# A four-layer graph network in float32: merging feature chunks for half of the nodes, two rows at a time

## The chip, the cores and the metric

The kernel runs on one core of one Trainium2 chip. The core has a matrix engine (TensorE, PE in the profile), a vector engine (VectorE, DVE), a scalar engine (ScalarE, ACT), a general one (GpSimd, POOL) and a queue for transfers (SyncE, SP). They run side by side and wait for each other by semaphores. The metric is the device time of one execution in microseconds (us).

## The reference, cut to what matters

x holds 64 graphs of 256 nodes with 128 features. Each of four layers does x = x + f(relu(layernorm(x)), adj). The first is the costly one: it takes a LeakyReLU of 256 values for every pair of nodes.

```python
def _L0_gnn_ref(x, W, b_lin, a, bias):        # x: normalised nodes; W = bias = adj
    W1, W2 = (W[:, :F], W[:, F:])              # F = 128, 256 outputs
    s1 = jnp.einsum('bkf,ef->bke', x, W1)
    s2 = jnp.einsum('bkf,ef->bke', x, W2)
    pre = s1[:, :, None, :] + s2[:, None, :, :] + b_lin
    h = jnp.where(pre >= 0, pre, ALPHA * pre)  # ALPHA = 0.2
    e = jnp.einsum('bije,e->bij', h, a) + bias
    attn = jax.nn.softmax(e, axis=2)
    out = jax.nn.sigmoid(jnp.einsum('bij,bjf->bif', attn, x))
    return out
...
h = jnp.maximum(_layernorm(x, axis=-1), 0.0)
x = x + _L0_gnn_ref(h, adj, L0_gnn_b_lin, L0_gnn_a, adj)
```

Layers 1 and 2 are attention layers on the same nodes, layer 3 is a gated recurrent cell with five steps that multiplies by adj in each. All is float32.

## The kernel before, in words

**The pair values.** With 0.2 x taken out as a linear term, what is left of the LeakyReLU is 0.8 relu(s1 + s2 + b). The kernel scales the 256 features by |a| (in `w_p`), so each counts with weight +0.8 or -0.8. It sorts them by sign: `place` says where a feature goes, and places 2p and 2p + 1 become partition p of chunk 0 and of chunk 1. The two features of a pair then have one sign, but for one pair where the number of positive ones is odd. For a node i, a *tile* is 128 features x 256 nodes j. ACT makes it as relu(s2 + s1[i]) (L687), POOL and DVE as max(s2, -s1[i]) (L692, L669), which differs by a number that falls out of the softmax over j.

**Batches.** A graph's 256 nodes are 32 rows of 8: four groups g of 32 nodes in each of two blocks `ic` of 128. A *batch* is one chunk of one row: a buffer `r` of 4 x 2 tiles, 8 KB on each partition, of which there are `BUFS` = 11. TensorE multiplies it by the signs: four matmuls (L740) side by side, one for each g, of 128 x 32 by 128 x 512, where the 512 are both blocks. `a_win` holds the signs in a window of zeros, so that row t of each group gets the sum. Every batch of a graph adds to the same bank `e_ps`.

**Merging.** Where five batches or more (`SPARE`) wait for TensorE as a row is begun (`Pairs.begin`), the row is *merged*: only chunk 0 is made, and DVE then makes chunk 1 of each of the eight tiles and adds it onto chunk 0 in one instruction, max(s2, -s1) + r (L709, in `merge`). TensorE has one batch to multiply instead of two. This needs one sign for both features of a pair. In the odd pair, the feature that has the place n_pos, in chunk 1, therefore gets size 0 in the permutation (`a_abs1`), and its part comes back by a rank-one correction: a matmul `left_ps`, and min(left, bound) + adj into `adj_l` (L570), one instruction for each block, which softmax0 then adds (L755).

**The order of work** is written out by a planner inside the kernel (`Model`, `Chain` and the loop at the end). It keeps a clock for each of PE, DVE, ACT and POOL, with fixed costs (a tile 365 ns on ACT and 454 on POOL, 2198 for DVE's eight, 1131 for its four, a merge 392, a batch 858), and issues next whatever can start first. Tiles are handed out in half batches to whichever of ACT, POOL and DVE is free and finds a buffer. All other work comes in chains: `ahead` (norms, s1, s2 and corrections of the next graphs), `behind` (softmax of the graph before), `chain12` (layers 1 and 2), `chain3` (layer 3; chains 4 and 5 for the last two groups). A chain's steps are spaced by a pace, 2400 ns for layer 3, until the last two graphs are begun. Each engine runs its instructions in the order written.

**Groups and transfers.** Graphs go in groups of two (one in the first two and last two groups). `load_x` fetches a group's x into one of five buffers, three groups ahead, from `begin`. SP holds all loads of x, the stores of the outputs, and the small transfers of the corrections' bounds, in order.

```python
merged = waiting >= SPARE
for ec in range(1 if merged else 2):
    batch = {"t": self.row, "ec": ec, "merged": merged, "halves": 0, "ready": 0.0}
    self.todo += [(batch, ec, 0), (batch, ec, 1)]
self.row += 1
```

Of the kernel before, what the change touches and what calls it, by code (L numbers as in the profile page):

```python
# [8 lines left out]
F32 = mybir.dt.float32  # L9
# [7 lines left out]
FLT_MAX = 3.4028234663852886e38  # L17
STEPS = 5
INV_SQRT_D = 1.0 / (128.0 ** 0.5)
BUFS = 11  # L20
SPARE = 5
MARGIN = {"pe": 300}
LANDS = 3400
# [32 lines left out]
def kernel(ctx: ExitStack, tc: tile.TileContext, ins: dict, out: bass.AP):  # L56
# [69 lines left out]
        return t[firsts[g] : firsts[g] + GROUPS[g]].rearrange("b (c p) f -> p (b c) f", p=P)  # L126

    def load_x(g):
        xt = ap.tile([P, 2 * GROUPS[g], P], F32, tag="xt", name="xt", bufs=5)
        nc.sync.dma_start(out=xt, in_=of_group(x, g))  # L130
        return xt

# [73 lines left out]
    bm_bc = fetch([P, P], "bm_bc", ins["L1_gnn_bm"].partition_broadcast(P))  # L206
    be_bc = fetch([P, 1], "be_bc", ins["L1_gnn_be"].partition_broadcast(P))
    biases = {k: column("L3_gnn_" + k) for k in ("w3_b", "u3_b", "w4_b", "w5_b", "u5_b")}
    xts.append(load_x(2))


    adj_t = constant([P, 2, N], "adj_t")
# [7 lines left out]
    def constants0():  # L220
# [34 lines left out]
        last, a_abs1 = col("last"), col("a_abs1")  # L255
        dve(2).tensor_scalar(last, place, n_pos, None, ALU.is_equal)
        dve(2).tensor_tensor(a_abs1, a_abs, last, ALU.mult)
        dve(2).tensor_tensor(a_abs1, a_abs, a_abs1, ALU.subtract)
        perm = lent([P, 2, 2, P], "perm", "e_t", 2)
        for src in range(2):  # L260
            for c, size in ((0, a_abs), (1, a_abs1)):
                dve(P).tensor_scalar(
                    perm[:, src, c, :], places[:, c, :], place[:, src : src + 1],
                    size[:, src : src + 1], ALU.is_equal, ALU.mult,
                )
        yield "pe"
        b_ps = psum([P, 2], "blin_ps")
# [50 lines left out]
        dve(1).tensor_copy(odd_all, p)  # L318
        left, left_n, left_nb = col("left"), col("left_n"), col("left_nb")
        dve(2).tensor_tensor(left, a_col, last, ALU.mult)  # L320
        dve(2).tensor_scalar(left, left, odd_all, 0.8, ALU.mult, ALU.mult)
        dve(2).tensor_scalar(left_n, left, -1.0, None, ALU.mult)
        dve(2).tensor_tensor(left_nb, left_n, blin, ALU.mult)
        for c in range(2):
# [105 lines left out]
    def ln_relu(space, xt, tag, ln, when=None, at=None):  # L430

        G = xt.shape[1]
        for g in range(G):
            if g % 2 == 0:
                yield "dve", when, at
            if g == 0:
                st = sp.tile([P, G, 6], F32, tag=tag + "_st", name="bst", bufs=2)
                mv = sp.tile([P, G, 2], F32, tag=tag + "_mv", name="bmv", bufs=2)
# [6 lines left out]
        ve = sp.tile([P, G], F32, tag=tag + "_ve", name="bve", bufs=2)  # L445
        minus = sp.tile([P, G], F32, tag=tag + "_mm", name="bmm", bufs=2)
        pool(277).tensor_scalar(ve, mv[:, :, 1], 1.0, LN_EPS, ALU.mult, ALU.add)
        pool(150).tensor_scalar(minus, mv[:, :, 0], -1.0, 0.0, ALU.mult, ALU.add)
        rstd = sp.tile([P, G], F32, tag=tag + "_rs", name="brs", bufs=2)
        pool(1085).tensor_tensor(rstd, ve, neg_half[:, 0:G], ALU.pow)  # L450
        shift = sp.tile([P, G], F32, tag=tag + "_sh", name="bsh", bufs=2)
# [81 lines left out]
    def bounds(of):  # L533


        yield "pe", lambda: counts["left"] > 0
        h_t = of["h_t"]
        G = h_t.shape[1]
        p = psum_h([P, P], "bound_ps")
        model.op("pe", P * 1.676)  # L540
        for c in range(G):
            nc.tensor.matmul(
                p[bass.ts(c, 32), :], lhsT=left_w, rhs=h_t[:, c, :], start=True, stop=True
            )
        yield "act"
        rows = sp.tile([P, P], F32, tag="rows", name="rows", bufs=2)
        act(P, 1).activation(
            rows[0 : 32 * G, :], p[0 : 32 * G, :], AF.Identity, bias=left_b[0 : 32 * G, :]
        )
        row = dp.tile([G, P], F32, tag="row", name="row")  # L550
        for c in range(G):
            nc.sync.dma_start(out=row[c : c + 1, :], in_=rows[32 * c : 32 * c + 1, :])
        bound = sp.tile([P, G], F32, tag="bound", name="bound")
        nc.sync.dma_start(out=bound, in_=row.rearrange("c p -> p c"))
        of["bound"] = bound
        of["bound_at"] = model.t["act"] + MEMORY

    def senders(b, of, to):
# [27 lines left out]
    class Pairs:  # L586

        def __init__(self, g, b, of, snd):
            self.g, self.b, self.of, self.snd = g, b, of, snd
            self.row = 0
# [6 lines left out]
            self.s1n_v = of["s1n"][:, :, bass.ts(b, N)].rearrange(  # L600
                "p c (k g t) -> p c g k t", k=2, g=4
            )

        def more(self):
            return self.todo or self.row < 32
# [4 lines left out]

        def begin(self):
            waiting = sum(x["halves"] == 2 for x in self.batches)
            merged = waiting >= SPARE
            for ec in range(1 if merged else 2):
                batch = {"t": self.row, "ec": ec, "merged": merged, "halves": 0, "ready": 0.0}
                self.todo += [(batch, ec, 0), (batch, ec, 1)]
            self.row += 1

        def finished(self):

# [21 lines left out]
            batch["halves"] += 1  # L642
            batch["ready"] = max(batch["ready"], model.t[who] + LAG[who])

        def nodes(self, t, g2):

            return [
                (g, ic, self.b * N + ic * P + 32 * g + t)
                for g in (2 * g2, 2 * g2 + 1) for ic in range(2)
            ]  # L650

        def make(self, who):
# [10 lines left out]
            if who == "dve":  # L663
                whole = g2 == 0 and self.todo and self.todo[0][0] is batch
                if whole:
                    self.todo.pop(0)
                n = 4 if whole else 2
                model.op("dve", model.WHOLE if whole else model.HALF)
                nc.vector.tensor_tensor(  # L669
                    r[:, 2 * g2 : 2 * g2 + n, :, :],  # L670
                    s2[:, ec : ec + 1, :].unsqueeze(1).to_broadcast([P, n, 2, N]),
                    self.s1n_v[:, ec, 2 * g2 : 2 * g2 + n, :, t : t + 1].to_broadcast([P, n, 2, N]),
                    ALU.max,
                )
                if whole:
# [25 lines left out]
        def merge(self):  # L701

            _, batch, g2 = self.merges.pop(0)
            r, t = batch["r"], batch["t"]
            for g, ic, i in self.nodes(t, g2):
                if g > 2 * g2 or ic:
                    yield
                model.op("dve", model.MERGE)
                nc.vector.scalar_tensor_tensor(  # L709
# [20 lines left out]
        def multiply(self):  # L730
# [5 lines left out]
            self.over = not self.batches and not self.more()  # L736
            t, r = batch["t"], batch["r"]
            model.op("pe", model.BATCH)
            for g in range(4):
                nc.tensor.matmul(  # L740
                    self.e_ps[bass.ts(g, 32), :, :].rearrange("p a b -> p (a b)"),
                    lhsT=a_win[:, batch["ec"], 31 - t : 63 - t], rhs=flat(r[:, g, :, :]),
                    start=False, stop=self.over, skip_group_check=True,
                )

    def softmax0(g, b, of, e_ps, snd):

# [2 lines left out]
        for ic in range(2):  # L750
            yield "dve", lambda: "adj_l" in snd

            if ic == 0:
                nmax = sp.tile([P, 2], F32, tag="nmax", name="nmax")
            dve(N, more=10).tensor_tensor_reduce(  # L755
                e_ps[:, ic, :], e_ps[:, ic, :], snd["adj_l"][:, ic, :], -1.0, FLT_MAX,
                ALU.add, ALU.min, nmax[:, ic : ic + 1],
            )
        for ic in range(2):
# [529 lines left out]
```

## Time and profile before

| | before |
|---|---|
| runs shown | 5033.29, 5038.96, 5039.4 us |
| median | 5038.96 us |
| the profiled execution | 5032.98 us, its span 5031.1 us |
| TensorE clock granted | 0.999 |
| matmuls of batches (L740) | 13912, of 512 columns each (27824 records) |
| tiles made by ACT / POOL | 10248 / 10100 |
| made by DVE (L669) | 659 of eight tiles, 551 of four |
| merges on DVE (L709) | 4944 |

How to read it: the page gives busy time and share of the span for each engine, and then groups of instructions by source line, with the number, the busy time, the mean time of one, and the time the engine stood idle just before them, with what ended it. Each float32 matmul leaves two records. ACT's and TensorE's instructions overlap their neighbours, so the mean time of one is longer than the step from one to the next. The table by stage gives busy time for each engine in a stretch of the span; the timeline gives the instructions in order of time, equal neighbours put together.

### The profile page before, as it was taken

The page shows a single profiled execution, that of the slowest core. Times are in us where ns is not written, and L with a number is a line of the kernel's source. Part 1 is how long each engine was busy: PE and PEld are TensorE (multiplying, and loading weights), DVE is VectorE, ACT ScalarE, POOL GpSimd, SP SyncE. Part 2 cuts the span into 40 slices and gives each one's busy share as a digit, 9 for nine tenths or more (in the row PEclk, how much of TensorE's full clock was granted, in tenths as well). Part 3 has the DMA queues.
Part 4 walks back from the last instruction along what each step waited for, and adds up shares of the span by engine and source line. Part 5 has one row for each costly group of instructions (what it writes and reads, how often), then busy time and mean ns, then how long its engine had stood idle before and what let it go on. Part 6 is the DMA issues. An engine that isn't in the chain of part 4 may idle for free. (4 is left out here: it accounts for less than half of the span.)

```text
span 5031.1 us, 151796 instructions
## 1 busy us (share of the span) xinstructions
PE 4975.7 (99%) x57307; PEld 1949.9 (39%) x57307; DVE 4926.9 (98%) x9026; ACT 4945.2 (98%) x12984; POOL 4817.0 (96%) x10725
## 2 busy tenths in 40 slices
PE   9999999999999999999999999999999999999998
PEld 3334433333334333343333333333333443333433
DVE  9999999999999999999999999999999999999995
ACT  8999999999999999999999999999999999999995
POOL 8999999999999999999999999999999999999991
PEclk9999999999999999999999999999999999999999
DMA  0000000000000000000000000000000000000000
GB/s 23 4 5 2 5 6 6 6 2 6 6 6 6 2 6 6 6 6 2 6 6 6 6 2 6 6 6 6 4 6 6 6 4 3 5 4 4 4 4 8
DMA packets 56017, 28.02 MB, mean 6 GB/s; under 512 B 20336, under 2 KB 55280, under 8 KB 55280
## 3 DMA queue, kind: packets, MB, share of 16 engines
q1 hardware_dynamic: 54736, 18.04, 1.5%
q8 instruction: 449, 7.36, 0.6%
q14 instruction: 288, 2.36, 0.2%
q10 hardware_dynamic: 544, 0.26, 0.0%
HBM read 9.84 MB, written 8.45 MB: 4 GB/s over the span
## 5 line engine op out<-in xcount | busy, mean ns | idle before, releaser
L692 POOL TENSOR_SCALAR r<-s,s1n 128x256 f32<-128x256 f32 x10100 | 4567.7, 476 | 55.7 <-PE e_ps L740 28.0
L687 ACT ACTIVATE r<-s_act,s 128x256 f32<-128x256 f32 x9736 | 4360.0, 1073 | 4.6 <-PE e_ps L740 4.3
L740 PE MATMUL e_ps<-r,a_win 128*32 128x512 f32 x27824 | 3251.8, 593 | 8.8 <-DVE r L709 4.0
L669 DVE TENSOR_TENSOR r<-s_ps,s1n 128x2048 f32<-128x2048 f32 (+1 forms) x1210 | 2120.7, 1790 | 0.8 <-POOL r L692 0.8
L709 DVE SCALAR_TENSOR_TENSOR r<-s_ps,s1n,r 128x256 f32<-128x256 f32 x4944 | 2013.3, 471 | 0.2
L740 PEld LDWEIGHTS e_ps<-r,a_win 128*32 128x32 f32 x27824 | 918.8, 110 | 1721.4 <-issue 1290.3
L687 ACT ACTIVATE r<-s,s 128x256 f32<-128x256 f32 x512 | 318.8, 1234 | 0.0
L458 ACT ACTIVATE h<-x,bsh,brs 128x128 f32<-128x128 f32 x384 | 264.3, 1040 | 10.5 <-POOL bsh L452 5.0
L109 PE MATMUL m_ps<-adj_t,hn 128*32 128x256 f32 x4096 | 253.6, 381 | 1.1 <-ACT hn L1066 1.1
L1025 ACT ACTIVATE m_ps<-gate_ps,br 128x512 f32<-128x512 f32 (+1 forms) x170 | 194.7, 1145 | 14.2 <-PE gate_ps L109 13.1
L1045 ACT ACTIVATE hv_ps<-hv_ps,bh 128x512 f32<-128x512 f32 (+1 forms) x170 | 198.7, 1169 | 7.2 <-PE hv_ps L109 7.2
L1043 ACT ACTIVATE gate_ps<-gate_ps,bz 128x512 f32<-128x512 f32 (+1 forms) x170 | 203.8, 1200 | 1.1 <-PE gate_ps L109 1.1
L1015 ACT COPY m_t<-m_ps 128x512 f32<-128x512 f32 (+1 forms) x170 | 193.9, 1140 | 6.1 <-PE m_ps L109 5.6
L109 PEld LDWEIGHTS m_ps<-adj_t,hn 128*32 128x32 f32 x4096 | 140.0, 110 | 126.2 <-issue 46.1
L109 PE MATMUL gate_ps<-m_t,t_w_w 128*32 128x512 f32 (+1 forms) x1360 | 172.7, 572 | 2.6 <-ACT m_t L1015 2.2
L109 PE MATMUL gate_ps<-m_t,w_t 128*32 128x512 f32 (+1 forms) x1360 | 172.5, 568 | 2.5 <-ACT m_ps L1025 2.4
L109 PE MATMUL hv_ps<-rh,u_th 128*32 128x512 f32 (+1 forms) x1360 | 172.1, 567 | 2.1 <-DVE rh L1028 2.0
L109 PE MATMUL hv_ps<-m_t,t_w_w 128*32 128x512 f32 (+1 forms) x1360 | 172.4, 568 | 0.0
L1066 ACT COPY hn<-hn_ps 128x512 f32<-128x512 f32 (+1 forms) x136 | 153.2, 1127 | 8.7 <-PE hn_ps L116 8.6
L109 PE MATMUL gate_ps<-hf,u_t 128*32 128x512 f32 (+1 forms) x1088 | 141.9, 571 | 0.0
L109 PE MATMUL s_ps<-h0t,w_p 128*32 128x256 f32 (+1 forms) x1568 | 136.2, 446 | 1.2 <-ACT h0t L474 0.5
L450 POOL TENSOR_TENSOR brs<-bve,neg_half 128x4 f32<-128x4 f32 (+1 forms) x136 | 133.5, 982 | 0.0
(214 smaller groups left out, 4781.2 us busy)
## 6 DMA issues: line engine op xcount, KB each, us to landing
xt<-in_x_dram SPq DMA_DIRECT2D x30, 256.0 KB
out_dram<-y SPq DMA_DIRECT2D x30, 256.0 KB
row<-rows SPq DMA_DIRECT2D x128, 0.5 KB
xt<-in_x_dram SPq DMA_DIRECT2D x4, 128.0 KB
out_dram<-y SPq DMA_DIRECT2D x4, 128.0 KB
bound<-row SPq DMA_DIRECT2D x30, 2.0 KB
raw_L_gnn_w_w<-in_L_gnn_w_w_dram SPq DMA_DIRECT2D x3, 128.0 KB
adj_n<-in_adj_dram ACTq DMA_DIRECT2D x1, 256.0 KB
```

The costliest lines, as they stand in the source:

```text
L109: nc.tensor.matmul(out[bass.ts(c, 32), :], lhsT=lhsT[:, bass.ts(c, 32)], rhs=rhs, **flags)
L458: act(P, 2, 1).activation(h[:, g, :], xt[:, g, :], AF.Relu, bias=shift[:, g : g + 1], scale=rstd[:, g : g + 1],)
L669: nc.vector.tensor_tensor(r[:, 2 * g2 : 2 * g2 + n, :, :], s2[:, ec : ec + 1, :].unsqueeze(1).to_broadcast([P, n, 2, N]), self.s1n_v[:, ec ...
L687: nc.scalar.activation(r[:, g, ic, :], s2[:, ec, :], AF.Relu, bias=s1[:, ec, i : i + 1])
L692: nc.gpsimd.tensor_scalar(r[:, g, ic, :], s2[:, ec, :], FLT_MAX, s1n[:, ec, i : i + 1], ALU.min, ALU.max,)
L709: nc.vector.scalar_tensor_tensor(r[:, g, ic, :], self.own("dve")[:, 1, :], self.of["s1n"][:, 1, i : i + 1], r[:, g, ic, :], ALU.max, ALU.add,)
L740: nc.tensor.matmul(self.e_ps[bass.ts(g, 32), :, :].rearrange("p a b -> p (a b)"), lhsT=a_win[:, batch["ec"], 31 - t : 63 - t], rhs=flat(r[ ...
L1015: act(W).copy(m_t, m_ps)
L1025: act(W, 1).activation(t_r, g_ps, AF.Tanh, bias=br, scale=0.5)
L1043: act(W, 1).activation(t_z, g_ps, AF.Tanh, bias=bz, scale=0.5)
L1045: act(W, 1).activation(cand, hv_ps, AF.Tanh, bias=bh)
L1066: act(W).copy(hn, tp)
```

## The change

`BUFS` becomes 12. The space comes from x (four buffers, fetched two groups ahead), from `adj_l` (one block instead of two) and from small tiles with one buffer instead of two.

Merging is now done for the first block of nodes alone, and for two rows t and t + 1 at once. A merged pair of rows has three batches: chunk 0 of row t and chunk 0 of row t + 1, both blocks, onto whose first block DVE adds chunk 1 (four merges each); and one batch that holds chunk 1 of the second block for both rows. So eight merges still save one batch in four. A graph can merge at most half as much as before.

The odd pair's feature keeps its size. In the first block its chunk 1 always goes with chunk 0's sign, merged or not, and the correction (with 1.6 in place of 0.8) is made for that block alone. In the second block chunk 1 goes with its own sign, and needs none. So chunk 1 of a row that isn't merged has a different weight for each block, and is multiplied by eight matmuls of 256 columns in place of four of 512; so is the batch of two rows.

```diff
-BUFS = 11
+BUFS = 12
...
-        xt = ap.tile([P, 2 * GROUPS[g], P], F32, tag="xt", name="xt", bufs=5)
+        xt = ap.tile([P, 2 * GROUPS[g], P], F32, tag="xt", name="xt", bufs=4)
...
-    xts.append(load_x(2))
...
-        dve(2).tensor_tensor(a_abs1, a_abs, last, ALU.mult)
-        dve(2).tensor_tensor(a_abs1, a_abs, a_abs1, ALU.subtract)
...
-        dve(2).tensor_scalar(left, left, odd_all, 0.8, ALU.mult, ALU.mult)
+        dve(2).tensor_scalar(left, left, odd_all, 1.6, ALU.mult, ALU.mult)
...
-        for ic in range(2):
-            yield "dve", None, of["bound_at"]
-            if ic == 0:
-                adj_l = ap.tile([P, 2, N], F32, tag="adj_l", name="adj_l", bufs=3)
-            dve(N, 1).scalar_tensor_tensor(
-                adj_l[:, ic, :], p, of["bound"][:, 2 * b + ic : 2 * b + ic + 1], adj_n[:, ic, :],
-                ALU.min, ALU.add,
-            )
+        yield "dve", None, of["bound_at"]
+        adj_l = ap.tile([P, N], F32, tag="adj_l", name="adj_l", bufs=3)
+        dve(N, 1).scalar_tensor_tensor(
+            adj_l, p, of["bound"][:, 2 * b : 2 * b + 1], adj_n[:, 0, :], ALU.min, ALU.add
+        )
...
-            merged = waiting >= SPARE
-            for ec in range(1 if merged else 2):
-                batch = {"t": self.row, "ec": ec, "merged": merged, "halves": 0, "ready": 0.0}
+            merged = waiting >= SPARE and self.row < 31
+            t = self.row
+
+            if merged:
+                kinds = ((t, 0, True, False), (t + 1, 0, True, False), (t, 1, False, True))
+            else:
+                kinds = ((t, 0, False, False), (t, 1, False, False))
+            for t, ec, on_top, two in kinds:
+                batch = {
+                    "t": t, "ec": ec, "merged": on_top, "two": two, "halves": 0, "ready": 0.0
+                }
                 self.todo += [(batch, ec, 0), (batch, ec, 1)]
-            self.row += 1
+            self.row += 2 if merged else 1
...
-            for g, ic, i in self.nodes(t, g2):
-                if g > 2 * g2 or ic:
+            for g, ic, i in self.nodes(batch, g2):
+                if ic:
+                    continue
+                if g > 2 * g2:
                     yield
                 model.op("dve", model.MERGE)
...
-            for g in range(4):
-                nc.tensor.matmul(
-                    self.e_ps[bass.ts(g, 32), :, :].rearrange("p a b -> p (a b)"),
-                    lhsT=a_win[:, batch["ec"], 31 - t : 63 - t], rhs=flat(r[:, g, :, :]),
-                    start=False, stop=self.over, skip_group_check=True,
-                )
+
+            if batch["two"]:
+                parts = ((1, t, 1, 0), (1, t + 1, 1, 1))
+            elif batch["ec"]:
+                parts = ((0, t, 0, 0), (1, t, 1, 1))
+            else:
+                parts = ((slice(0, 2), t, 0, slice(0, 2)),)
+            for ic, t, sign, k in parts:
+                for g in range(4):
+                    to, of = self.e_ps[bass.ts(g, 32), ic, :], r[:, g, k, :]
+                    if len(parts) == 1:
+                        to, of = to.rearrange("p a b -> p (a b)"), flat(of)
+                    nc.tensor.matmul(
+                        to, lhsT=a_win[:, sign, 31 - t : 63 - t], rhs=of,
+                        start=False, stop=self.over, skip_group_check=True,
+                    )
...
-            if g + 3 < len(GROUPS):
-                xts.append(load_x(g + 3))
+            if g + 2 < len(GROUPS):
+                xts.append(load_x(g + 2))
```

Left out of the diff: the eight small statistics tiles and `rows` with one buffer instead of two, the views of s1 for a batch of two rows in `nodes` and `make`, and the reads of `adj_n` in place of `adj_l` for the second block in `softmax0`.

More of the change, by code (lines that the diff above doesn't have):

```diff
@@ L253, in constants0 @@
         dve(2).tensor_tensor(place, dif, neg_pl, ALU.add)
-        last, a_abs1 = col("last"), col("a_abs1")
+        last = col("last")
         dve(2).tensor_scalar(last, place, n_pos, None, ALU.is_equal)
-        dve(2).tensor_tensor(a_abs1, a_abs, last, ALU.mult)
-        dve(2).tensor_tensor(a_abs1, a_abs, a_abs1, ALU.subtract)
         perm = lent([P, 2, 2, P], "perm", "e_t", 2)
         for src in range(2):
-            for c, size in ((0, a_abs), (1, a_abs1)):
+            for c in range(2):
                 dve(P).tensor_scalar(
                     perm[:, src, c, :], places[:, c, :], place[:, src : src + 1],
-                    size[:, src : src + 1], ALU.is_equal, ALU.mult,
+                    a_abs[:, src : src + 1], ALU.is_equal, ALU.mult,
                 )
@@ L436, in ln_relu @@
             if g == 0:
-                st = sp.tile([P, G, 6], F32, tag=tag + "_st", name="bst", bufs=2)
-                mv = sp.tile([P, G, 2], F32, tag=tag + "_mv", name="bmv", bufs=2)
+                st = sp.tile([P, G, 6], F32, tag=tag + "_st", name="bst", bufs=1)
+                mv = sp.tile([P, G, 2], F32, tag=tag + "_mv", name="bmv", bufs=1)
             dve(P).bn_stats(st[:, g, :], xt[:, g, :])
@@ L443, in ln_relu @@
         yield "pool"
-        ve = sp.tile([P, G], F32, tag=tag + "_ve", name="bve", bufs=2)
-        minus = sp.tile([P, G], F32, tag=tag + "_mm", name="bmm", bufs=2)
+        ve = sp.tile([P, G], F32, tag=tag + "_ve", name="bve", bufs=1)
+        minus = sp.tile([P, G], F32, tag=tag + "_mm", name="bmm", bufs=1)
         pool(277).tensor_scalar(ve, mv[:, :, 1], 1.0, LN_EPS, ALU.mult, ALU.add)
         pool(150).tensor_scalar(minus, mv[:, :, 0], -1.0, 0.0, ALU.mult, ALU.add)
-        rstd = sp.tile([P, G], F32, tag=tag + "_rs", name="brs", bufs=2)
+        rstd = sp.tile([P, G], F32, tag=tag + "_rs", name="brs", bufs=1)
         pool(1085).tensor_tensor(rstd, ve, neg_half[:, 0:G], ALU.pow)
-        shift = sp.tile([P, G], F32, tag=tag + "_sh", name="bsh", bufs=2)
+        shift = sp.tile([P, G], F32, tag=tag + "_sh", name="bsh", bufs=1)
         pool(302).tensor_tensor(shift, minus, rstd, ALU.mult)
@@ L545, in bounds @@
         yield "act"
-        rows = sp.tile([P, P], F32, tag="rows", name="rows", bufs=2)
+        rows = sp.tile([P, P], F32, tag="rows", name="rows", bufs=1)
         act(P, 1).activation(
@@ L602, in __init__ @@
             )
+            self.s1n_b = of["s1n"][:, :, bass.ts(b, N)].rearrange(
+                "p c (k g t) -> p c k g t", k=2, g=4
+            )
         def more(self):
@@ L643, in whole, with nodes @@
             batch["ready"] = max(batch["ready"], model.t[who] + LAG[who])
-        def nodes(self, t, g2):
+        def nodes(self, batch, g2):
+            t, two = batch["t"], batch["two"]
             return [
-                (g, ic, self.b * N + ic * P + 32 * g + t)
-                for g in (2 * g2, 2 * g2 + 1) for ic in range(2)
+                (g, k, self.b * N + 32 * g + t + (P + k if two else k * P))
+                for g in (2 * g2, 2 * g2 + 1) for k in range(2)
             ]
@@ L667, in make @@
                 n = 4 if whole else 2
+                if batch["two"]:
+                    s1n = self.s1n_b[:, ec, 1, 2 * g2 : 2 * g2 + n, t : t + 2].unsqueeze(3)
+                else:
+                    s1n = self.s1n_v[:, ec, 2 * g2 : 2 * g2 + n, :, t : t + 1]
                 model.op("dve", model.WHOLE if whole else model.HALF)
@@ L671, in make @@
                     s2[:, ec : ec + 1, :].unsqueeze(1).to_broadcast([P, n, 2, N]),
-                    self.s1n_v[:, ec, 2 * g2 : 2 * g2 + n, :, t : t + 1].to_broadcast([P, n, 2, N]),
+                    s1n.to_broadcast([P, n, 2, N]),
                     ALU.max,
@@ L703, in merge @@
             _, batch, g2 = self.merges.pop(0)
-            r, t = batch["r"], batch["t"]
-            for g, ic, i in self.nodes(t, g2):
-                if g > 2 * g2 or ic:
+            r = batch["r"]
+            for g, ic, i in self.nodes(batch, g2):
+                if ic:
+                    continue
+                if g > 2 * g2:
                     yield
@@ L738, in multiply @@
             model.op("pe", model.BATCH)
-            for g in range(4):
-                nc.tensor.matmul(
-                    self.e_ps[bass.ts(g, 32), :, :].rearrange("p a b -> p (a b)"),
-                    lhsT=a_win[:, batch["ec"], 31 - t : 63 - t], rhs=flat(r[:, g, :, :]),
-                    start=False, stop=self.over, skip_group_check=True,
-                )
+            if batch["two"]:
+                parts = ((1, t, 1, 0), (1, t + 1, 1, 1))
+            elif batch["ec"]:
+                parts = ((0, t, 0, 0), (1, t, 1, 1))
+            else:
+                parts = ((slice(0, 2), t, 0, slice(0, 2)),)
[7 more added lines that the diff above has]
+                        start=False, stop=self.over, skip_group_check=True,
+                    )
     def softmax0(g, b, of, e_ps, snd):
@@ L755, in softmax0 @@
             dve(N, more=10).tensor_tensor_reduce(
-                e_ps[:, ic, :], e_ps[:, ic, :], snd["adj_l"][:, ic, :], -1.0, FLT_MAX,
+                e_ps[:, ic, :], e_ps[:, ic, :], adj_n[:, 1, :] if ic else snd["adj_l"], -1.0, FLT_MAX,
                 ALU.add, ALU.min, nmax[:, ic : ic + 1],
```

## The prediction

> **What bounds the kernel now.** I read the page first. All four engines are over 95% busy, so no engine is "the" bound by its share, and the chain that ended last says only how the last 94 us go. The question is which engine has real slack, and where.
>
> ```profile
> PE 4975.7 (99%) x57307; PEld 1949.9 (39%) x57307; DVE 4926.9 (98%) x9026; ACT 4945.2 (98%) x12984; POOL 4817.0 (96%) x10725
> ...
> L692 POOL TENSOR_SCALAR r<-s,s1n 128x256 f32<-128x256 f32 x10100 | 4567.7, 476 | 55.7 <-PE e_ps L740 28.0
> L687 ACT ACTIVATE r<-s_act,s 128x256 f32<-128x256 f32 x9736 | 4360.0, 1073 | 4.6 <-PE e_ps L740 4.3
> L740 PE MATMUL e_ps<-r,a_win 128*32 128x512 f32 x27824 | 3251.8, 593 | 8.8 <-DVE r L709 4.0
> ...
> L709 DVE SCALAR_TENSOR_TENSOR r<-s_ps,s1n,r 128x256 f32<-128x256 f32 x4944 | 2013.3, 471 | 0.2
> ```
>
> Three engines make tiles (L692, L687, L669), DVE also merges (L709), TensorE multiplies (L740). The makers hardly ever wait: 28.0 us on POOL for a free buffer, 4.3 on ACT, 0.2 before a merge.
>
> Busy time overlaps on TensorE and ACT, so for both I take the step from one instruction to the next, from the timeline:
>
> ```profile
> 2499.41 2.33 PE L740 MATMUL e_ps<-r,a_win 128*32 128x512 f32 x20
> 2502.26 3.64 PE L740 MATMUL e_ps<-r,a_win 128*32 128x512 f32 x32
> ...
> 2505.72 1.91 PE L109 MATMUL m_ps<-adj_t,hn 128*32 128x256 f32 x32
> ...
> 2508.30 0.61 PE L109 MATMUL th_ps<-xh_t,wt_rep 128*32 128x256 f32 x8
> ```
>
> Four matmuls run side by side (one per 32 columns), and each f32 matmul has two records. 12 more records, three more such passes, take 3.64 - 2.33 = 1.31 us: a pass of 512 columns costs 0.43 us, a batch (4 matmuls, two passes) 0.86. With 256 columns, 24 more records, six passes, take 1.91 - 0.61 = 1.30: 0.216 us each, half of 0.43 to within 1%. ACT's 44 tiles in a row from 37.60 us take 15.91 us, 0.36 each; POOL's 4567.7 / 10100 is 0.45; DVE's steps are 2.20 (a 128x2048 tile), 1.13 (half of one) and 0.39 (a merge).
>
> With these steps TensorE's own work is 4881 us: 27824 / 4 passes of 0.43 for the batches (2991, or 2984 at the finer 0.429), and about 1900 for all other matmuls and transposes. So of the span it idles 150 us: some 20 in the first 157 us, 28 in the last 94, and about 100 in between, 1.6 us for each of the 64 graphs. The makers idle some 2 us in each 157 us, by the same count. Makers are the bound of the body, TensorE is 2% behind them.
>
> Except at the end:
>
> ```profile
> 17.00:4443.00 4426.00, 4397.95 (x50276) 1713.76 (x50272) 4394.18 (x7881) 4418.14 (x11629) 4342.56 (x9652) 1.00 0.02 5
> ...
> 4676.00:4937.00 261.00, 260.87 (x3188) 106.39 (x3184) 258.20 (x619) 249.50 (x643) 236.63 (x530) 1.00 0.02 5
> 4937.00:5031.00 94.00, 75.85 (x1059) 36.17 (x1051) 36.03 (x88) 39.32 (x93) 4.42 (x14) 0.96 0.03 7
> ```
>
> In the table by stage (PE, PEld, DVE, ACT, POOL), the last three graphs (from 4676) show TensorE busy 260.87 of 261 us while ACT falls to 249.5 and POOL to 236.6: here layer 3, which is paced in the body, catches up, and TensorE is the bound. After 4937 the last graph runs alone through its layers.
>
> **The change, part by part.** The two programs' instruction orders differ in few counts; everything else is equal to the instruction.
>
> Tiles: ACT makes 72 fewer (-72 x 0.36 = -26 us), POOL 88 fewer (-88 x 0.45 = -40). DVE makes 738 whole tiles for 659 (+79 x 2.20 = +174), 543 halves for 551 (-9), 4504 merges for 4944 (-440 x 0.39 = -172), and 64 corrections (L570, one block in place of two) for 128 (-64 x 0.39 = -25): -32. Each maker loses 0.5 to 0.8% of its work.
>
> TensorE: 440 merges fewer are 55 batches more, 55 x 0.86 = +47. And 11880 matmuls are of 256 columns (2970 side-by-side fours, two passes each, 1.5 us more per thousand passes than two halves should cost, 0.216 against 0.2145): +9. Together +57 us, 4938.
>
> Here the Trainium skill speaks against the change. The page "TensorE: Matmul & The Clock Gate", section "Back-to-back issue gap", gives 81 ns per matmul at 128 columns and 131 ns at 512 in a stream of weight loads and matmuls, so narrow matmuls would be far from proportional; an estimate between the two, 98 ns at 256, would make two halves 1.5 times a whole and put some 600 us on the changed matmuls. The rows above, with weight loads in the stream, show 1% instead, and the sum goes by them.
>
> Where does this leave the time? Counted only up to the last batch of graph 60 (of 0 to 63; 4676 us in the profile), the makers' work changes by -34 us (ACT), -34 (POOL), -31 (DVE) and TensorE's by +37. If the makers stay the bound, that point comes 31 us earlier. The order has a clock in it that tells the same: layer 3 is issued by a chain with a fixed pace, and its outputs come evenly,
>
> ```profile
> 1624.83 0.68 DVE L1075 TENSOR_TENSOR y<-y_ps,x 128x512 f32<-128x512 f32 x1
> ...
> 4606.41 0.68 DVE L1075 TENSOR_TENSOR y<-y_ps,x 128x512 f32<-128x512 f32 x1
> ```
>
> 19 groups apart, 156.9 us per group, though a group of graphs takes 154. Before the last batch of graph 58 the order of before has 5404 matmuls of layer 3, that of after 5364. A group has 200, so graph 58 ends 40 / 200 x 156.9 = 31 us earlier on that clock; at graph 22 the two are equal, at 37 they are 36 apart, at 60 still 40. ACT's layer-3 instructions (658 and 653, 24 in a group) say 33, DVE's (548 and 544, 20 in a group) 31. For this, TensorE may idle only 53 us up to graph 60 where it now idles 121, the first 20 in it. I take -31.
>
> The last three graphs: TensorE is the bound, and the relief is smaller. Before merges all that it can, 152 + 136 + 144; after, with half the nodes open to merging, 104 + 112 + 112. 104 merges fewer are 13 batches, 11 us; with the 256-column extra and a bit more of layer 3 left over, TensorE's work from graph 60's last batch to graph 63's rises from 260.2 to 275.5 us. With no idle time to give: +15. Its bounds are 0 (if the makers were still the bound there; the row denies it) and +15.
>
> The tail after the last batch: 4.7 us more TensorE work on 76 busy of 94. Bounds 0 and +5, taken +2.
>
> Twelve buffers in place of eleven: POOL's 28.0 us and ACT's 4.3 on TensorE bound the gain; part of the -31 already, since the order is made with them. As a gain of its own 0 to -10, taken 0.
>
> x two groups ahead: 34 loads as before, each one group later on SP, behind the same kind of output store. A load is still issued a whole group, 154 us, before its first reader. SP's longest wait for an output is 136.7 us, so even a load stuck behind it arrives; behind the load stand the transfers of the next corrections' bounds, 7 us before their use at most by the planner, and they stood behind the same stores before. Statistics tiles with one buffer are reused a group later. Both 0, hidden under that group; without that cover, one stall of up to some 20 us per group would show at once. The start loses two DVE instructions of 0.1 us: nothing.
>
> Sum: -31 + 15 + 2 = -14 us. The profiled execution took 5032.98 us (span 5031.1, 1.9 around it), so 5019; the median of the runs before, 5038.96, is 6.0 above it, so I forecast 5025 on that scale.
>
> **The rivals.**
>
> *TensorE becomes the bound of the body* (slower). It has 37 us more to do up to graph 60, and the idle time there is partly waits in its queue that nothing in the change removes: a correction matmul (left_ps) waiting for DVE to let go of a bank, the last halves of a graph, small waits for POOL and ACT. If the 121 us shrink only to 90, graph 60 comes at +6 and the kernel ends at 6 + 17 = +23: 5062. If none goes, +37 + 17 = +54: 5093. It decides from 77 us of idle on (where the total is +10). For it: DVE r and left_ps waits in the rows of TensorE are real, and two engines without slack stumble over each other. Against it: stretches of 157 us in the trace with 1.0 to 1.4 us of TensorE idle show no more idle makers than others, and the last 261 us show TensorE without any.
>
> *The gain is eaten, but no more*: stumbling of 0.2 us per graph, 12 us, on -14: 5037, no change.
>
> *The end hides its 15 us too*: layer 3's catch-up fits beside the makers, and the whole -31 to -33 stays: 5007.
>
> *x comes late*: 20 us in each of 32 groups would be +600; SP's row of waits speaks against it, and I give it 1 in 100.
>
> **How the numbers follow.** A run-to-run difference of 0.2%, 10 us, is about what a measurement can tell from no change. The forecast case gets 0.42 (5015 to 5035 by itself), the whole gain 0.13, the eaten gain 0.19, TensorE as bound 0.25, x late 0.01. Faster than 5029 is most of the first (0.36) and the second: 0.49. Within 10 us of 5039: the rest of the first, the eaten gain, and a little of the TensorE case: 0.26. Slower: 0.25. The range reaches from the whole gain with a little luck, 5004, to the TensorE case at 90 us of idle, 5062; it leaves out the upper part of that case and little below.
>
> **What would show it.** Right: graph 60 ends near 4645; from there to the last batch about 276 us with TensorE full; POOL's wait for TensorE in the body well under 28 us; 256-column passes at 0.216; DVE merges 4504 x 0.39; outputs of layer 3 still 157 apart in the body. Wrong: idle before L764's weight loads as large as before with POOL and ACT waiting on TensorE (the TensorE case), a pass of 256 columns above 0.23, bn_stats waiting for the load of x, or the last three graphs as short as 261 us.

## The result, and the profile after

The changed kernel takes 5020.28 us (median of 7 runs, 5019.59 to 5023.06), where before takes 5038.88 in the same comparison: a ratio of 0.9965, 95% interval 0.9954 to 0.9975. In a second comparison it was 5017.90 against 5031.61, 0.9973 (0.9963 to 0.9984). So it is faster by 0.3%, 14 to 19 us. The forecast was 5025, 14 us less than the median before.

The page of the changed kernel, its engines and the groups that answer to those shown of before:

```profile
PE 4985.7 (99%) x69627; PEld 2291.3 (46%) x69627; DVE 4895.7 (98%) x8591; ACT 4922.9 (98%) x12912; POOL 4778.0 (95%) x10637
...
L703 POOL TENSOR_SCALAR r<-s,s1n 128x256 f32<-128x256 f32 x10012 | 4528.5, 476 | 79.4 <-PE e_ps L764 36.4
L698 ACT ACTIVATE r<-s_act,s 128x256 f32<-128x256 f32 x9664 | 4170.7, 871 | 7.6 <-PE e_ps L764 6.0
L764 PE MATMUL e_ps<-r,a_win 128*32 128x256 f32 (+1 forms) x40144 | 3258.1, 467 | 3.4 <-DVE r L680 3.3
...
L722 DVE SCALAR_TENSOR_TENSOR r<-s_ps,s1n,r 128x256 f32<-128x256 f32 x4504 | 1852.6, 471 | 1.7 <-POOL r L703 1.0
```

The span is 5017.8 us for 5031.1. TensorE's share is what it was, 99%, and that says nothing. Its records went from 27824 to 40144, but 23760 of these have half the columns; counted in 512 columns they are 28264, for the 440 merges that DVE has fewer to make. The makers still hardly wait. POOL waits longer for TensorE to free a buffer, 36.4 us for 28.0, though it has one buffer more; the rise is in the last three graphs (17.6 us for 6.6), while up to graph 61 it waits 18.8 us for 21.4.

The table by stage (PE, PEld, DVE, ACT, POOL), cut at the same points of the work as before: up to shortly before graph 60, the last three graphs, the tail:

```profile
17.00:4412.00 4395.00, 4388.42 (x61329) 2015.84 (x61331) 4365.04 (x7514) 4385.93 (x11534) 4310.78 (x9581) 1.00 0.02 6
4645.00:4922.00 277.00, 277.00 (x3798) 124.95 (x3788) 253.45 (x542) 256.28 (x655) 230.10 (x514) 1.00 0.02 5
4922.00:5018.00 96.00, 78.27 (x1112) 37.85 (x1108) 38.53 (x95) 41.69 (x98) 5.67 (x18) 0.95 0.03 7
```

The last three graphs take 277 us instead of 262, with TensorE busy for all of it. Graph 61 starts (its first matmul into a new bank) at 4644.6 us instead of 4675.7. The tail is 95.8 us instead of 93.5. So -31.1 + 15.5 + 2.3 = -13.3 us, the difference of the two spans.

Layer 3's outputs keep their clock, as the timeline has them, 19 groups apart again:

```profile
1625.73 0.67 DVE L1098 TENSOR_TENSOR y<-y_ps,x 128x512 f32<-128x512 f32 x1
...
4606.23 0.67 DVE L1098 TENSOR_TENSOR y<-y_ps,x 128x512 f32<-128x512 f32 x1
```

156.9 us per group, to the tenth what it was, while the graphs went by 0.7% faster. Layer 3 falls further behind them, and more of it is left for the end.

One more number is used below: *TensorE's idle*, counted as in the prediction from the trace (the stretch from the start of graph 4 to that of graph 61, less the steps of all the matmuls in it, with the same steps for every run). It is 97.8 us before and 30.2 after.

### The profile page after: what moved, and what is told of

Read it like the earlier page. It is cut to its first block, busy times and chain, and to the rows that moved or that the text cites. A ratio compares the mean times of both kernels' runs of the same rounds, so it can differ in the third digit from the quotient of the medians.

```text
span 5017.8 us, 176085 instructions
## 1 busy us (share of the span) xinstructions
PE 4985.7 (99%) x69627; PEld 2291.3 (46%) x69627; DVE 4895.7 (98%) x8591; ACT 4922.9 (98%) x12912; POOL 4778.0 (95%) x10637
## 4 chain that ended last, share of the span: by engine, by line
PE 92%; DVE 4%; ACT 3%; issue 1%; POOL 0%; DMA 0%; DVEq 0%; ACTq 0%; POOLq 0%
PE e_ps L764 56%; PE gate_ps L109 8%; PE hv_ps L109 6%; PE m_ps L109 5%; PE s_ps L109 3%; DVE r L680 3%; PE o_ps L109 2%; PE e_ps L109 2%; ACT r L698 2%; PE rc_ps L109 2%; PE hn_ps L116 1%; PE rsum_ps L109 1%; PE e_ps L116 1%; PE h_t_ps L116 1%; DVE r L722 1%
## 5 line engine op out<-in xcount | busy, mean ns | idle before, releaser
L703 POOL TENSOR_SCALAR r<-s,s1n 128x256 f32<-128x256 f32 x10012 | 4528.5, 476 | 79.4 <-PE e_ps L764 36.4
L698 ACT ACTIVATE r<-s_act,s 128x256 f32<-128x256 f32 x9664 | 4170.7, 871 | 7.6 <-PE e_ps L764 6.0
L764 PE MATMUL e_ps<-r,a_win 128*32 128x256 f32 (+1 forms) x40144 | 3258.1, 467 | 3.4 <-DVE r L680 3.3
L680 DVE TENSOR_TENSOR r<-s_ps,s1n 128x1024 f32<-128x1024 f32 (+1 forms) x1281 | 2291.0, 1824 | 3.9 <-PE e_ps L764 3.9
L764 PEld LDWEIGHTS e_ps<-r,a_win 128*32 128x32 f32 x40144 | 1279.9, 110 | 1574.3 <-issue 853.6
L722 DVE SCALAR_TENSOR_TENSOR r<-s_ps,s1n,r 128x256 f32<-128x256 f32 x4504 | 1852.6, 471 | 1.7 <-POOL r L703 1.0
L455 ACT ACTIVATE h<-x,bsh,brs 128x128 f32<-128x128 f32 x384 | 229.6, 850 | 5.6 <-POOL bsh L449 4.7
L1066 ACT ACTIVATE gate_ps<-gate_ps,bz 128x512 f32<-128x512 f32 (+1 forms) x170 | 170.8, 1005 | 2.7 <-PE gate_ps L109 2.7
L1038 ACT COPY m_t<-m_ps 128x512 f32<-128x512 f32 (+1 forms) x170 | 161.4, 949 | 9.3 <-PE m_ps L109 9.3
L1048 ACT ACTIVATE m_ps<-gate_ps,br 128x512 f32<-128x512 f32 (+1 forms) x170 | 161.0, 949 | 8.9 <-PE gate_ps L109 7.2
```

The source lines that it names most:

```text
L455: act(P, 2, 1).activation(h[:, g, :], xt[:, g, :], AF.Relu, bias=shift[:, g : g + 1], scale=rstd[:, g : g + 1],)
L680: nc.vector.tensor_tensor(r[:, 2 * g2 : 2 * g2 + n, :, :], s2[:, ec : ec + 1, :].unsqueeze(1).to_broadcast([P, n, 2, N]), s1n.to_broadcast ...
L698: nc.scalar.activation(r[:, g, ic, :], s2[:, ec, :], AF.Relu, bias=s1[:, ec, i : i + 1])
L703: nc.gpsimd.tensor_scalar(r[:, g, ic, :], s2[:, ec, :], FLT_MAX, s1n[:, ec, i : i + 1], ALU.min, ALU.max,)
L722: nc.vector.scalar_tensor_tensor(r[:, g, ic, :], self.own("dve")[:, 1, :], self.of["s1n"][:, 1, i : i + 1], r[:, g, ic, :], ALU.max, ALU.add,)
L764: nc.tensor.matmul(to, lhsT=a_win[:, sign, 31 - t : 63 - t], rhs=of, start=False, stop=self.over, skip_group_check=True,)
```

## The experiments

The theory is the prediction's: in the body the makers of tiles set the time, at the end TensorE does. Rivals: TensorE alone is the bound everywhere; twelve buffers are the gain; the pairs are the gain. Each span is that of one profiled execution; the ratios are of timed runs, each against before in the same comparison, estimated from all timed runs, so that they can differ from the quotient of two medians by 0.0002. POOL's wait is that of the whole kernel.

| run | ratio to before (95%) | graph 61 starts | last three graphs | tail | span | TensorE's idle | POOL waits for TensorE |
|---|---|---|---|---|---|---|---|
| before | 1 | 4675.7 | 261.9 | 93.5 | 5031.1 | 97.8 | 28.0 |
| changed | 0.9965 (0.9954-0.9975) | 4644.6 | 277.4 | 95.8 | 5017.8 | 30.2 | 36.4 |
| e0 changed again | 0.9973 (0.9963-0.9984) | 4644.9 | 277.4 | 92.6 | 5014.9 | 30.2 | 37.8 |
| e1 eleven buffers | 0.9984 (0.9975-0.9993) | 4651.0 | 275.4 | 93.9 | 5020.4 | 29.7 | 55.4 |
| e3 memory alone | 1.0000 (0.9991-1.0009) | 4676.0 | 261.9 | 93.6 | 5031.5 | 98.3 | 27.5 |
| e4 rows at the end | 0.9955 (0.9942-0.9969) | 4644.8 | 267.9 | 94.0 | 5006.6 | 30.2 | 28.1 |
| e5 wide matmuls | 0.9968 (0.9957-0.9980) | 4641.3 | 277.3 | 97.3 | 5015.9 | 32.0 | 31.0 |
| e6 merge from four | 0.9979 (0.9970-0.9988) | 4654.5 | 273.8 | 97.1 | 5025.4 | 57.4 | 18.4 |
| e7 merge from six | 0.9988 (0.9980-0.9997) | 4657.1 | 281.0 | 93.6 | 5031.7 | 29.7 | 47.4 |
| e8 correction twice | 0.9991 (0.9982-1.0000) | 4654.0 | 275.9 | 95.5 | 5025.5 | 28.7 | 42.7 |
| e9 pairs alone | 0.9993 (0.9985-1.0002) | 4657.7 | 275.2 | 93.7 | 5026.6 | 29.3 | 54.6 |
| e10 faster pace | 0.9976 (0.9966-0.9986) | 4675.0 | 256.7 | 84.9 | 5016.5 | 29.4 | 37.3 |
| e12 no late merges | 0.9989 (0.9980-0.9998) | 4673.1 | 266.3 | 95.8 | 5035.2 | 73.7 | 22.8 |
| e13 chunk 1 first | 0.9979 (0.9970-0.9988) | 4648.7 | 275.9 | 101.9 | 5026.5 | 35.4 | 34.6 |

The median of before is 5031.6 to 5038.9 us from one comparison to the next, so medians are set side by side within one comparison, or as ratios. The changed kernel's two profiled spans differ by 2.9 us, all of it in the tail; the starts of graph 61 agree to 0.3.

Four rows need care. POOL's busy time for one tile is 454.6 or 454.7 ns in e6, e7, e12 and e13, and 452.2 to 452.4 in all other traces, before and changed among them; for the 9600 tiles that POOL makes up to graph 61 that is 22 us. The four were measured in two comparisons on other chips, where 41 of 42 executions of before take 5035.8 us or more; beside the other e runs 48 of 49 take 5034.1 or less. So some 7 us in the starts and spans of these four can come from there, and the changed kernel was not run in these comparisons. Their ratios are the fairer measure.

### The changed kernel again

> The changed kernel once more, so that it stands beside the others on one chip: a ratio of 0.9965 to before, as measured.

The same kernel in one comparison with e3, e9 and e10: 0.9973, inside the first interval. Its trace repeats the body and the last three graphs to 0.3 us.

### The memory edits alone

```diff
-        xt = ap.tile([P, 2 * GROUPS[g], P], F32, tag="xt", name="xt", bufs=5)
+        xt = ap.tile([P, 2 * GROUPS[g], P], F32, tag="xt", name="xt", bufs=4)
...
-    xts.append(load_x(2))
...
-            if g + 3 < len(GROUPS):
-                xts.append(load_x(g + 3))
+            if g + 2 < len(GROUPS):
+                xts.append(load_x(g + 2))
```

(and one buffer for the statistics tiles and `rows`)

> The kernel before with the change's edits to memory alone: x in four buffers and fetched two groups ahead, statistics tiles and rows with one buffer; eleven buffers of tiles, merging as before. The order of all engines but SP is the same to the instruction. If x is hidden and nobody waits for a statistics tile: a ratio of 1.000 to before. Rival 'the later fetch or the single buffers cost, and hide part of the gain': 1.001 or more.

1.0000, and every column of the table is before's to 0.5 us. What paid for the twelfth buffer in x and the small tiles cost nothing that can be measured.

### Eleven buffers

```diff
-BUFS = 12
+BUFS = 11
```

> The changed kernel with eleven buffers instead of twelve, all else as changed. Makers bound (my theory): the work counts stay within 0.2% of the changed kernel's, but the clock of layer 3 in the order puts graph 58 at 22 us before the old kernel instead of 31; so 9 us slower than the changed kernel, near 5029, 10 faster than before. Rival 'twelve buffers are the gain': all of it goes, near 5039. Rival 'buffers are nothing, merging is all': near 5020.

Graph 61 starts 6.4 us later, the span is 2.6 longer, the ratio 0.9984. Beside the changed kernel's other trace, whose tail is shorter, the span is 5.5 longer. That is between the first theory and the third: the order's clock had promised 9 us in the body, and of the 6.4 that came, 2.0 come back in the last three graphs; what the tail adds or takes is within what it varies. What the twelfth buffer is for stands in POOL's waits (engine, line, releaser: sum, times, longest), here of this run

```profile
POOL r L703 <- PE e_ps L764: 55.4, 32, 4.5
```

where the changed kernel has 36.4. Up to graph 61 it is 36.1 us here and 18.8 there.

### The correction made twice

```diff
+        yield "dve"
+        dve(N, 1).scalar_tensor_tensor(
+            adj_l, p, of["bound"][:, 2 * b : 2 * b + 1], adj_n[:, 0, :], ALU.min, ALU.add
+        )
```

> The changed kernel with the correction instruction on DVE made twice for each graph (the same values again), so that DVE does as many as before: 64 x 0.39 = 25 us more on DVE. Makers bound: the planner spreads it over the three makers, whose work up to graph 60 is 6 to 9 us more than in the changed kernel: 6 to 9 us slower, near 5028. Rival 'TensorE is the bound of the body, the makers have slack': 0, 5020. Rival 'DVE alone is the bound': +25, 5045.

Graph 61 starts 9.4 us later, the span is 7.7 longer, the ratio 0.9991. Neither 0 nor 25: a DVE instruction more is paid at about a third of its time, since the planner hands tiles to the other makers and merges less. This is the second part of the gain: the block that needs no correction saves 8 to 9 us.

### Pairs alone

Both of the last two edits together:

```diff
-BUFS = 12
+BUFS = 11
...
+        yield "dve"
+        dve(N, 1).scalar_tensor_tensor(
+            adj_l, p, of["bound"][:, 2 * b : 2 * b + 1], adj_n[:, 0, :], ALU.min, ALU.add
+        )
```

> The changed kernel with eleven buffers and the correction made twice: of the change's gains only the merging of pairs is left, with its 256-column matmuls. By the traces of the two single runs (start of graph 61 later by 6.4 and 9.4 us, span by 2.6 and 7.7 us), if the parts add: graph 61 starts 15 us earlier than before, the last three graphs take 14 us longer than before, and the span is 5028, a ratio of 0.9995. Rival 'the parts overlap, pairs are the gain': 5020, 0.998.

Graph 61 starts 18.0 us before the old kernel's (15 expected), the last three graphs take 13.3 longer, the span is 5026.6, the ratio 0.9993 with 1 inside its interval. The parts add, nearly. So pairs by themselves gain 18 us in the body and lose 13 of them at the end; buffers and correction make the difference that can be measured.

But one column moved at once: TensorE's idle is 29.3 us already here. The pairs took it from 98 to 30, not the buffers (29.7 with eleven).

### Fewer or more merges

```diff
-SPARE = 5
+SPARE = 4
```

> The changed kernel, merging from four waiting batches on instead of five: 208 merges more. Up to graph 60 TensorE's work is 18 us less than in the changed kernel, the makers' 9 to 15 us more. If the makers bound the body too: graph 61 starts 9 to 14 us later, in total 5 to 12 us slower than the changed kernel. Rival 'TensorE alone is the bound of the changed body': 10 to 18 us faster.

```diff
-SPARE = 5
+SPARE = 6
```

> The changed kernel, merging from six waiting batches on: 120 merges fewer. Up to graph 60 TensorE's work is 15 us more than in the changed kernel, the makers' 7, 9 us less (ACT, POOL) and 2 more (DVE). If TensorE's 30 us of idle over graphs 4 to 60 are as few as it can have: graph 61 starts 10 to 15 us later, in total 8 to 16 us slower. Rival 'the makers alone are the bound, as I predicted': 0 to 7 us faster.

These two say who is the bound. With 120 merges fewer, graph 61 starts 12.5 us later, and TensorE's idle is 29.7 us, what it is in the changed kernel: the 15 us of work that it has more account for the delay, so TensorE is the bound. With 208 merges more, TensorE has 18 us less to do and idles 57.4 us, and graph 61 starts 9.9 us later: the makers are the bound. How much of the 9.9 is their 9 to 15 us of added work and how much the longer POOL time there was not separated. The makers' groups by line and shape (number, busy time and mean, idle before and what ended it), first with four, then with six:

```profile
L703 POOL TENSOR_SCALAR r<-s,s1n 128x256 f32<-128x256 f32 x10056 | 4571.6, 485 | 53.8 <-PE e_ps L764 18.4 <-DVE v_rep L299 9.2 <-DVE r L722 2.8
L698 ACT ACTIVATE r<-s_act,s 128x256 f32<-128x256 f32 x9688 | 4391.1, 1124 | 7.9 <-PE e_ps L764 7.7
```

```profile
L703 POOL TENSOR_SCALAR r<-s,s1n 128x256 f32<-128x256 f32 x9988 | 4541.3, 484 | 98.5 <-PE e_ps L764 47.4 <-DVE v_rep L299 9.9 <-issue 9.4
L698 ACT ACTIVATE r<-s_act,s 128x256 f32<-128x256 f32 x9624 | 4164.5, 887 | 17.0 <-PE e_ps L764 16.6
```

Four and six show POOL's longer time here: 485 and 484 ns on average, where the changed kernel's line has 476. Up to graph 61 POOL waits 8.9 us for a buffer with four, 18.8 with five and 20.2 with six, ACT 0.3, 2.0 and 8.1. So the changed kernel stands near where the two limits meet. By the ratios six costs time (0.9988, with both ratios of the changed kernel below its interval), while four (0.9979) can't be told from the changed kernel's 0.9973. "The makers alone are the bound" falls, as it had six at least as fast as five, and so does "TensorE alone", which had four faster by 10 us or more: a ratio of 0.9953 at most, outside four's interval.

### Wide matmuls

```diff
-            elif batch["ec"]:
-                parts = ((0, t, 0, 0), (1, t, 1, 1))
             else:
-                parts = ((slice(0, 2), t, 0, slice(0, 2)),)
+                parts = ((slice(0, 2), t, batch["ec"], slice(0, 2)),)
```

> The changed kernel, but chunk 1 of a row that isn't merged is multiplied by four matmuls of 512 columns, with one sign for both blocks (the first block's chunk 1 of the odd pair then has the wrong sign there, so this part of the result is changed); instruction order otherwise the same. TensorE's work falls by 5.5 us by the 1% that a split costs. Makers bound: 0 to -2 us, near 5019. Rival 'TensorE is the bound of the body': -5 us, 5015. Rival 'narrow matmuls cost much more than half': several tens of us faster.

Graph 61 starts 3.3 us earlier, for 5.5 us less of TensorE's work; the span is 1.9 less, within what the tail varies, and the ratio 0.9968 can't be told from the changed kernel's. Between the first two expectations, as for two limits that meet. In the changed kernel's trace two passes of 256 columns that follow each other in L764 start 0.216 us apart (the median of 4572). Narrow matmuls cost 1% more than half.

### Rows again at the end

The last two graphs merge whole rows: both blocks take chunk 0's sign, and both are corrected.

```diff
+FULL = 2
...
-            merged = waiting >= SPARE and self.row < 31
+            full = self.snd["full"]
+            merged = waiting >= SPARE and (full or self.row < 31)
...
-            if merged:
+            if merged and full:
+                kinds = ((t, 0, True, False),)
+            elif merged:
...
-            self.row += 2 if merged else 1
+            self.row += 2 if merged and not full else 1
...
-                if ic:
+                if ic and not self.snd["full"]:
                     continue
...
-            elif batch["ec"]:
+            elif batch["ec"] and not self.snd["full"]:
...
+    sent = [{"full": k >= len(graphs) - FULL} for k in range(len(graphs))]
```

(with a second correction tile, in a buffer that x no longer needs by then)

> The changed kernel, but the last two graphs merge whole rows (both blocks, one row at a time, chunk 1 with chunk 0's sign in both blocks, the correction made for both). If TensorE is the bound in the last three graphs, its work there falls from 275.5 to 263.7 us and the kernel ends 10 to 12 us earlier, near 5009, although the makers get more work (DVE +12 us, POOL +5). Rival 'makers are the bound to the end': 0 to +6 us, 5020 to 5026.

Up to graph 61 the trace is the changed kernel's. Then:

```profile
4645.00:4913.00 268.00, 267.17 (x3406) 112.74 (x3398) 264.69 (x634) 252.14 (x647) 235.51 (x527) 1.00 0.02 5
4913.00:5007.00 94.00, 76.47 (x1108) 37.50 (x1108) 38.27 (x95) 41.70 (x98) 5.68 (x18) 0.97 0.03 7
```

The last three graphs take 267.9 us instead of 277.4, with DVE at 264.7 of 268 us instead of 253.5 of 277. 9.5 us less, and 5006.6 of span: 5008.42 us where before took 5032.03 in the same comparison, 0.9955. The makers had room at the end, TensorE had none. This version is the fastest of all: by medians 9.5 us below the changed kernel's 5017.90 in e0, measured beside a before of 5031.61, nearly the same.

### A faster pace for layer 3

```diff
-    ahead, behind, chain3, chain12 = Chain(1500), Chain(2500), Chain(2400), Chain(2200)
+    ahead, behind, chain3, chain12 = Chain(1500), Chain(2500), Chain(2300), Chain(2200)
```

> The changed kernel with a pace of 2300 ns in place of 2400 for layer 3, so that it no longer falls behind the graphs (65 steps x 2.3 = 149.5 us a group, less than the 153 a group of graphs takes). If the last three graphs are long because layer 3 catches up there on a full TensorE, they take 15 to 20 us less (about 258 in place of 277), and graph 61 starts 15 to 20 us later, since the makers' work up to graph 60 is 17 to 24 us more: the end time moves by -6 to +3. Rival 'the end is long for the smaller relief alone': 277 to 272 us there, and the whole 12 or more slower.

The last three graphs take 256.7 us instead of 277.4 and the tail 84.9 instead of 95.8, while graph 61 starts 30.4 us later (15 to 20 expected): layer 3's work has moved forward, where TensorE has no room either. In total 1.3 us less than the changed kernel by span and 5018.82 to 5017.90 us by medians of one comparison: no difference that can be measured. So layer 3's catch-up is what makes the end long, and moving it does not pay; merging more against it does.

### Why TensorE's idle went

```diff
-            merged = waiting >= SPARE
+            merged = waiting >= SPARE and self.row < 28
```

on the kernel before:

> The kernel before, but rows 28 to 31 of a graph are never merged. Theory: the old rule leaves TensorE idle at the end of each graph, where its last batches still wait for eight merges on DVE, while the next graph's batches may not start; then TensorE's idle time over graphs 4 to 60 falls from 98 us to 60 or less, graph 61 starts 10 to 20 us earlier with TensorE's work up to there 22 us more and the makers' 7 to 15 less, and the ratio to before is 0.997 to 0.999. Rival 'it is the pairs as such (three batches at a time), not when the merges come': idle stays above 85 us, and with 25 us more work for TensorE the kernel is 0 to 10 us slower, 1.000 to 1.002.

Idle falls from 97.8 to 73.7 us, between the two expectations; graph 61 starts 2.6 us earlier, though POOL takes longer in this trace. The ratio of the timed runs is 0.9989 with an interval below 1, 5.4 us by medians. That the profiled span is 4.1 us longer than before's says nothing against it, since before's trace has the shorter POOL time, and beside e12 before took some 7 us longer. Late merges are a part of the idle: 24 of 68 us by these two traces, and what the longer POOL time adds to the idle of this one isn't known.

On the changed kernel, the pair's batch without merges first:

```diff
-                kinds = ((t, 0, True, False), (t + 1, 0, True, False), (t, 1, False, True))
+                kinds = ((t, 1, False, True), (t, 0, True, False), (t + 1, 0, True, False))
```

> The changed kernel with the three batches of a merged pair made in another order: the one without merges (chunk 1 of the second block) first, the two that wait for merges last. Theory 'TensorE's idle time went because a pair ends with a batch that needs no merge': idle over graphs 4 to 60 rises from 30 us to 50 or more and graph 61 starts 10 us or more later. Rival 'what counts is that a batch waits for four merges and not for eight, and that a pair commits three batches': idle stays near 30, graph 61 starts within 5 us of the changed kernel's 4645. The counts (4512 merges, TensorE's work up to graph 60 0.3 us less) and the clock of layer 3 (31 us at graph 58, as in the changed kernel) speak for the second.

Idle is 35.4 us, graph 61 starts 4.1 us later, no more than the longer POOL time can make: the sequence inside a pair is not it. (The tail is 101.9 us, the longest of all; why stays open.) What the idle of before had to do with is seen in its own trace: of some 100 us of idle between two passes that fall into graphs 1 to 62, 32 lie in the last tenths of the graphs, where with pairs alone it is 5. In the 2 to 8 us before the next graph's first matmul, DVE makes 3.6 merges per graph before and 1.3 with pairs. A row with eight merges holds its batch back twice as long as one with four, and the next graph's batches may not start. But more of the fall lies earlier: in the fifth to ninth tenths of the graphs the idle goes from 48 us to 15, two thirds of that before the matmuls of layer 3 and the transposes. No run shows why; the end of a graph explains less than half of what the pairs do to TensorE's idle.

## Why the prediction was right, point by point

**The bound.** "Makers are the bound of the body, TensorE is 2% behind them" was right of the kernel before (97.8 us idle, 2.2%). For the changed kernel the working went on as if the makers were the only limit, and asked of TensorE that its idle up to graph 60 fall from 121 us to 53. It fell to exactly that (4644.6 - 4591.8 = 52.8 by the same count), but it had little further to fall: over graphs 4 to 60 no run has less than 28.7 us, and e7, with 15 us more work for TensorE, has 29.7. The forecast landed on the point where both limits meet.

**-31 up to graph 60.** Measured -31.1. Both ways to it held: the makers' counts (-34, -34, -31) and the clock of layer 3 in the order. The second could be trusted because the outputs come 156.9 us apart in both traces. For e1 the same clock said 9 us and 6.4 came, for e6 9 and 9.9, for e7 9 and 12.5, for e8 0 and 9.4: it moves in lumps of one layer-3 step or two, and is good to some 10 us (in e6 and e7 with the longer POOL time in what came), so the hit to 0.1 us is luck.

**+15 in the last three graphs.** Measured +15.5. e4 shows the cause: merge as before there, in two of the three graphs, and 9.5 us come back; e10 shows that layer 3's catch-up is what fills TensorE there. The bound of 0 from below, "if the makers were still the bound there", is excluded.

**+2 in the tail.** +2.3 in one execution and -0.9 in the other, so 0 within what the tail varies.

**Twelve buffers, "0 to -10 as a gain of its own, taken 0, part of the -31 already".** They are worth 6.4 us in the body and 2.6 or 5.5 in the span, by which of the changed kernel's traces is taken, and it is in the -31, as the order is made with them. The sign that the prediction gave for it, POOL's wait for TensorE in the body well under 28 us, came as worded, 18.8 us, but says little: the 28.0 was the whole kernel's wait, and before's in the body is 21.4. With eleven buffers it is 36.1, so the fuller TensorE makes POOL wait longer, and the twelfth buffer takes that back in the body. In the last three graphs the wait rose from 6.6 us to 17.6, which the prediction did not foresee.

**x, and the small buffers: 0.** e3, a ratio of 1.0000. No bn_stats waits for x beyond the first (1.6 us).

**Narrow matmuls: 1%.** 0.216 us a pass. An estimate from the two figures that the Trainium skill gives, page "TensorE: Matmul & The Clock Gate", section "Back-to-back issue gap", would have had them cost half as much again; e5 takes back 1844 of the 2970 fours of narrow matmuls and gains 3.3 us up to graph 61. For these float32 passes, four side by side, the trace decides against that estimate.

**The rivals.** "TensorE becomes the bound of the body" had to keep 77 us of its 121 us of idle: it kept 53. It was nearer than its chance made it look, since TensorE did become a bound of the body, only with far less idle, and the prediction had no reason for why the idle should go. The reason is known only in part: e9 shows that the fall comes with the pairs alone, e12 that late merges are a share of it, and the rest is open. "The end hides its 15 us too" is excluded by the table by stage. "The gain is eaten" is excluded by both intervals.

**The sum.** -14 forecast; -13.3 by the spans, -13.7 by the medians of the second comparison, -18.6 by those of the first, whose interval (-12.6 to -23.2) takes in all of these. On the scale of the profiled executions the forecast was 5019, and 5019.59 came. The 6.0 us that the prediction put on top, to get from before's profiled execution to its median, did not carry over: the changed kernel's median is 0.7 above its profiled execution, and that is the 5 us by which 5025 was too high. The -18.6 sets it beside a before of which six runs in seven took 5038.5 us or more; the two values near -13.5 have before at its lower level.

## What to carry to other kernels

When a planner keeps several engines full, a change is worth the work that it takes off the engine that is the limit, and no more than the slack of the next one: count each engine's work and idle from the steps in the trace before and after, by stage, since busy shares of 98% say nothing. Work that is paced by a clock of its own shows in the instruction order how much earlier a point comes, before anything is run, here to some 10 us. Before two traces are set side by side, compare the step of one and the same instruction in both: 0.5% on one engine is as large here as the effects that were looked for. And look at the last stage by itself: what is put off in the body comes due there, where a scheme with less relief costs most, and where the old scheme for the last two graphs of 64 was worth 9.5 us, where the whole change is worth 13 by the spans.

## What the runs showed of the hardware

A pass of four float32 matmuls side by side takes 0.216 us at 256 columns and 0.429 at 512, with a new weight load for each matmul, also in a stream of 11880 of them: no price for the smaller size beyond 1%. And TensorE could be kept at work for 99.3% of 4350 us (30.2 us idle) and for the last 277 us without a gap in its busy time, at a granted clock of 0.999, while its makers waited for it no more than 1% of the time. The same POOL instruction took 452.2 to 452.4 ns of busy time for a tile in ten traces and 454.6 or 454.7 in four others, from comparisons on other chips in which the kernel before took some 7 us of 5032 longer; that the one makes the other was not shown.
